# A first FFN product in 26 block products with streamed weight sums

## The chip, the cores and the metric

The kernel runs on one core of a Trainium2 chip. The core has five queues that matter here: TensorE (PE, matmuls into PSUM), VectorE (DVE), ScalarE (ACT), GpSimd (POOL), and SyncE (SP), which issues nearly all of the DMAs. Each works through its own instructions in the order of the program, and semaphores tie them together. The metric is the device time of one execution in microseconds (us). Everything is computed in float32.

## The reference, cut to what matters

The block normalises x and adds an attention branch and a feed-forward branch to it:

```python
xn = _layernorm(x, axis=-1)                                  # x: 8 x 1024 x 256
qkv = (xn @ qkv_w + qkv_b).reshape(b, n, 3, 16, 16)
q, k = _l2norm(q), _l2norm(k)
kv = jnp.einsum('bhnd,bhne->bhde', k, v)
out = jnp.einsum('bhnd,bhde->bhne', q, kv)                   # no softmax
attn = out @ proj_w + proj_b
h = jax.nn.relu(jnp.einsum('bsh,hi->bsi', xn, W1) + b1)      # W1: 256 x 1024
ffn = jnp.einsum('bsi,ih->bsh', h, W2) + b2                  # W2: 1024 x 256
return x + attn + ffn
```

The change is about h = relu(xn @ W1 + b1), which has 1024 tokens, 256 inputs and 1024 outputs in each of eight batches.

## The kernel before, in words

The eight batches go through a pipeline. For batch b the program does four things on TensorE, one after the other:

- `hidden(b)` (L646) forms h. This product and most of the others are done by a scheme of the Strassen and Winograd kind: a product of 2 x 2 blocks is formed from seven block products in place of eight. The blocks of x are two halves of the inputs by two halves of the tokens, `xnT`, plus the sums s1, s2 and s4 in `xS` and s3, which is formed in place (L221). The weights are `w1_sb` and their sums `w1t`. Four groups of 128 + 128 outputs, seven products each, make 28 block products of 512 columns a batch (L658). VectorE adds partial products from PSUM (L670), ScalarE applies relu with the bias (L665), GpSimd then forms the sums of h that the next product needs (`sums_of_a`, L190).
- `project_by_sums(b + 1)` (L399) forms q and k of the next batch in 14 block products of two 256-column matmuls each (`pqa`, `pqc`, `pqd`, `pqe`, L415).
- `second(b)` (L789) forms the output: seven products of five matmuls each, over the four groups of h and, as a fifth, the attention branch folded to a 256 x 256 matrix M times q. Results go through VectorE (`join`, `turn_back`) and are added to the rows of x in `xq` by GpSimd (L821), which SyncE then stores.
- Between the first four and the last three products of `second(b)` stands `mix_g_by_sums(b + 1)` (L577; `gpa`, `gpc`, `gpd`, `gpe`), the product of x and k of the next batch. Its sums are formed by GpSimd in `g_sums` (L545), in three parts.

Two small products, `mix_kv` (L613, `kvp`) and `mix_m` (L632, `mp`), stand inside `hidden`.

While that goes on, batch b + 2 is prepared: `norm_stats`, `norm_scale`, `norm_apply` (L274, eight instructions on ScalarE) and `turn_x` (L302), which transposes x with four 32 x 32 block transposes on VectorE and 16 DMAs on SyncE. `turn_q` (L494) does the same for q. Both use one buffer named turn. `norms_of_q` (L473) forms the norms of q and `scale` (L486) applies them.

The order is written by hand: `tc.manual_schedule()` keeps every engine's instructions in the order in which the Python code emits them, and a small table (`later_steps`, L760) says behind which step of `hidden` other work is emitted. The framework adds the waits. SyncE's queue follows that order too. Before, it ran in each batch: 16 DMAs of `turn_x`, eight stores, eight loads of `xq`, two loads of x, 16 DMAs of `turn_q`.

Seven PSUM banks are shared by all products (`bank`, L90), an eighth serves the small products.

## Time and profile before

| | |
|---|---|
| runs shown | 611.4, 611.2 and 610.72 us, median 611.2 |
| span of the profiled execution | 608.3 us |
| what lies around the span | 2.4 to 3.1 us, taken from the runs (the profiled execution's own time is not listed apart from its span) |
| TensorE busy | 604.2 us, 99% of the span |
| VectorE, ScalarE, GpSimd busy | 419.8, 208.0, 422.1 us |
| DMA | 45.42 MB, 75 GB/s on average |
| granted TensorE clock | 1.000 |
| one batch in the middle | 74.2 us (from 251.91 to 326.08), of which `hidden` 25.8 |

The stages of batch 3 on TensorE, read from the chain of work in order of time: `hidden` from 251.91 to 277.70, `project_by_sums(4)` to 289.79, the first four products of `second(3)` to 306.96, the mix of batch 4 to 313.21, the last three products to 326.08. In a line of the profile, `x10` counts instructions, two for each float32 matmul; "SPq" marks DMA issues on SyncE's queue; a time in square brackets is what the engine waited before and for whom.

### The profile page before, as it was taken

Reading aid. Unit: us, or ns where it says so; the run is one execution under the profiler, and the core shown is the slowest. Engines: PE = TensorE matmul, PEld = TensorE weight load, DVE = VectorE, ACT = ScalarE, POOL = GpSimd, SP = SyncE. Lnnn points to the kernel's source line nnn. Section 1 sums busy time; section 2 is a strip of 40 time slices with the busy share of each in tenths; the row PEclk is TensorE's granted clock in tenths of the full one; section 3 lists DMA queues with packets and bytes.
Section 4 is the critical chain, followed back from the end, with each engine's and each line's share of the span. In section 5 each row is a group of like instructions: output and inputs, shape, how many; then the busy total and the mean of one; then the engine's idle time right before and its main releaser. Section 6 shows DMA issues by size and latency. Waiting matters only on the chain.

```text
span 608.3 us, 6773 instructions
## 1 busy us (share of the span) xinstructions
PE 604.2 (99%) x2049; PEld 349.1 (57%) x2049; DVE 419.8 (69%) x754; ACT 208.0 (34%) x362; POOL 422.1 (69%) x346
## 2 busy tenths in 40 slices
PE   9999999999999999999999999999999999999998
PEld 5466664565644756447464484644846447554446
DVE  6987667877487774787647875577846878257854
ACT  4644214441334413343133531435205262023500
POOL 2899992699636995479944899249991599923900
PEclk9999999999999999999999999999999999999999
DMA  8543403840048300581005810159001550005313
GB/s 287 88 101 75 99 1 71 167 108 0 1 98 190 59 1 2 120 185 41 0 13 127 178 31 0 24 118 193 13 0 36 128 114 1 1 1 123 84 21 84
DMA packets 150068, 45.42 MB, mean 75 GB/s; under 512 B 145936, under 2 KB 147088, under 8 KB 150032
## 3 DMA queue, kind: packets, MB, share of 16 engines
q1 hardware_dynamic: 146528, 43.84, 32.4%
q10 hardware_dynamic: 3504, 1.15, 0.8%
q8 instruction: 16, 0.26, 0.2%
q14 instruction: 20, 0.16, 0.1%
HBM read 20.32 MB, written 8.39 MB: 47 GB/s over the span
## 4 chain that ended last, share of the span: by engine, by line
PE 99%; DVE 0%; issue 0%
PE poa L784 11%; PE poe L784 11%; PE pod L784 10%; PE pha L658 9%; PE phe L658 9%; PE phd L658 9%; PE poc L784 6%; PE phc L658 5%; PE pqd L415 4%; PE pqe L415 4%; PE pqa L415 4%; PE pq L326 2%; PE gpd L588 2%; PE gpe L588 2%; PE gpa L588 2%; PE pqc L415 2%
## 5 line engine op out<-in xcount | busy, mean ns | idle before, releaser
L821 POOL TENSOR_TENSOR xq<-xq,yt_o 128x512 f32<-128x512 f32 x29 | 36.8, 1269 | 119.5 <-DVE yt_o L816 119.5
L665 ACT ACTIVATE hT<-hT,b_sb 128x512 f32<-128x512 f32 x96 | 69.0, 722 | 61.3 <-DVE hT L670 56.2
L192 POOL TENSOR_TENSOR hS<-hT 128x512 f32<-128x512 f32 x31 | 46.5, 1500 | 32.5 <-ACT hT L665 32.5
L658 PE MATMUL pha<-xnT,w_sb 128*128 128x512 f32 x128 | 65.4, 592 | 0.0
L393 ACT ACTIVATE sq<-qk 128x512 f32<-128x512 f32 x56 | 34.2, 627 | 83.8 <-DVE qk L421 69.2
L784 PE MATMUL poa<-hT,w_sb 128*128 128x512 f32 x128 | 57.6, 592 | 0.0
L670 DVE TENSOR_TENSOR hT<-phe,u 128x512 f32<-128x512 f32 x64 | 43.7, 685 | 7.0 <-PE phe L658 5.2
L194 POOL TENSOR_TENSOR hS<-hT,hS 128x512 f32<-128x512 f32 x31 | 39.6, 1276 | 2.4
L193 POOL TENSOR_TENSOR hS<-hS,hT 128x512 f32<-128x512 f32 x31 | 39.5, 1274 | 2.4
L196 POOL TENSOR_TENSOR hT<-hT 128x512 f32<-128x512 f32 x31 | 39.9, 1289 | 0.0
L784 PEld LDWEIGHTS poa<-hT,w_sb 128*128 128x128 f32 x128 | 23.8, 190 | 24.2 <-issue 23.9
L658 PEld LDWEIGHTS pha<-xnT,w_sb 128*128 128x128 f32 x128 | 23.7, 190 | 22.9 <-issue 22.2
L670 DVE TENSOR_TENSOR u<-phc,u 128x512 f32<-128x512 f32 x32 | 21.7, 679 | 20.2 <-ACT u L684 11.0
L665 ACT ACTIVATE hT<-pha,b_sb 128x512 f32<-128x512 f32 x32 | 21.8, 683 | 35.5 <-PE pha L658 35.5
L816 DVE STREAM_TRANSPOSE yt_o<-y_o 128x512 f32<-128x512 f32 x29 | 31.7, 1093 | 2.9 <-ACT y_o L953 0.6
L658 PE MATMUL phc<-xS,w1t 128*128 128x512 f32 x64 | 32.7, 592 | 0.0
L658 PE MATMUL phd<-xnT,w_sb 128*128 128x512 f32 x64 | 32.7, 592 | 0.0
L658 PE MATMUL phd<-xnT,w1t 128*128 128x512 f32 x64 | 32.7, 592 | 0.0
L658 PE MATMUL phe<-xS,w_sb 128*128 128x512 f32 x64 | 32.7, 592 | 0.0
L658 PE MATMUL phe<-xS,w1t 128*128 128x512 f32 x64 | 32.7, 592 | 0.0
L684 ACT COPY u<-pha 128x512 f32<-128x512 f32 x32 | 18.4, 575 | 35.5 <-PE pha L658 35.5
L784 PE MATMUL poe<-hS,w2t 128*128 128x512 f32 x64 | 28.8, 592 | 0.0
(192 smaller groups left out, 1323.3 us busy)
## 6 DMA issues: line engine op xcount, KB each, us to landing
qT<-turn_q SPq DMA_DIRECT2D x128, 64.0 KB, 2.1
x<-in_L_attn_x_dram SPq DMA_DIRECT2D x15, 512.0 KB, 5.6
xq<-in_L_attn_x_dram SPq DMA_DIRECT2D x60, 128.0 KB, 3.7
out_dram<-xq SPq DMA_DIRECT2D x58, 128.0 KB, 2.7
xnT<-turn_x SPq DMA_DIRECT2D x112, 64.0 KB, 2.1
w_sb<-in_L_ffn_W_dram SPq DMA_DIRECT2D x2, 512.0 KB, 7.1
w_sb<-in_L_ffn_W_dram SPq DMA_DIRECT2D x8, 128.0 KB, 3.5
x<-in_L_attn_x_dram SPq DMA_DIRECT2D x3, 256.0 KB, 6.0
```

Source lines behind the costliest of these rows:

```text
L192: eng.tensor_tensor(s1, a21, a22, ALU.add)
L193: eng.tensor_tensor(s2, s1, a11, ALU.subtract)
L194: eng.tensor_tensor(s4, a12, s2, ALU.subtract)
L196: eng.tensor_tensor(a21, a11, a21, ALU.subtract)
L393: nc.scalar.activation(sq, part_of_qk(b, n, g, m), AF.Square)
L415: nc.tensor.matmul(dst[:, w, :], a[:, g, :, w], rhs, start=start and w == 0, stop=stop, skip_group_check=True,)
L588: nc.tensor.matmul(dst, l[:, t, :], r[:, t, :], start=start and t == 0, stop=stop and t == HT - 1, skip_group_check=True,)
L658: nc.tensor.matmul(dst, lhsT, rhs, start=start, stop=stop, skip_group_check=True)
L665: nc.scalar.activation(block(i, n, m), src, AF.Relu, bias=b1_sb[:, fc : fc + 1])
L670: nc.vector.tensor_tensor(dst, p, q, ALU.add)
L784: nc.tensor.matmul(dst, l, r, start=start and n == 0, stop=stop and n == len(lhs) - 1, skip_group_check=True,)
L821: nc.gpsimd.tensor_tensor(xh, xh, yt.rearrange("p u w r c -> p (u w) r c"), ALU.add)
```

## The change

For batches 1 to 7 the first FFN product is computed by another scheme. W1 is cut into four blocks of 256 outputs by two of 128 inputs, x into two blocks of 128 inputs by four of 256 tokens; the 4 x 2 x 4 block product takes 26 block products, where 28 were used. A block product is now two matmuls of 256 columns, one for each 128 outputs. The table `PRODUCTS` lists, for each, the PSUM chain into which it is added, the sum of W1 blocks, and the sum of x blocks; `STEPS` lists in which order products, copies out of PSUM (ScalarE), additions (VectorE) and relus (`"R"`, ScalarE, two instructions each) are emitted. A chain's bank is read between its products, with the partial sum in it, and later products are added on top.

The 26 sums of W1 are formed once, during `second(0)`, on VectorE (19) and ScalarE (2), and stored in DRAM by 26 DMAs. From then on they are streamed: 13 pairs of 256 KB a batch, through five places in SBUF, ten products ahead at the start of `hidden` and the rest within it. The sums of x are formed by GpSimd: ten while `hidden` of the batch before runs, eight more (X3 to X10, kept in the place of k) after the mix. q and k are projected from seven of the same sums and the blocks of x, which needs three more sums of their weights. Batch 0 keeps its old scheme under the name `first_hidden`.

What else moves: in `second`, the products come in the order a, a, f, c, d, then the mix, then e, e, so that two products stand behind the mix where there were three; `join(1, 1)` stands behind the turn of x; `join(1, 0)` is emitted ahead of the last part of `g_sums`; the sums of h and q are formed after the whole of `hidden`; the loads of `xq` and x stand behind `hidden`; half of the stores move into the next batch's `hidden`. The bias of q and its scaling go from GpSimd and `hidden` into `norms_of_q` on VectorE, which moves ahead of the c product (for batch 1 it stays behind the turn of x).

The core of the diff:

```diff
+PRODUCTS = (
+    (23, "+21-22-31+32", "s3B"), (20, "+21", "b12"), (24, "+12", "b22"), (8, "+11", "b12"),
+    (1, "+22", "b22"), (24, "-12-21+41-42", "X3"), (4, "+21-22-41+42", "X1"),
+    (10, "+12+42", "s1A"), (11, "+41-42", "X2"), (7, "+12+32+42", "b23"),
+    (10, "-12-31-42", "s2A"), (11, "+21-41+42", "X4"), (12, "+31-32", "dA"),
...
+    (3, "-42", "X9"), (2, "+21-41", "X10"),
+)
+STEPS = (
+    0, 1, ("copy", 42, 20, 1), 2, ("add", 24, 42, "-", "B23"), ("copy", 12, 24, 1), 3, 4,
...
+    ("add", 41, "B11", "+", 41), ("R", 41), 16, ("add", 23, 23, "+", "B12"), ("copy", 14, 8, 1),
+    ("R", 23), 17, ("add", 34, "B3", "-", 14), 18, ("add", 32, "B1", "+", 34), ("R", 32), 19,
+    ("add", 24, "B12", "+", 24), ("R", 24), 20, ("add", 34, "B12", "+", 34), ("R", 34), 21,
...
+)
     def sums_of_wqk():
...
+        for dst, p, q in (
+            (wt[:, 0, :], b12, b11), (wt[:, 1, :], b22, wt[:, 0, :]), (t3, b22, b12),
+            (wt[:, 2, :], b21, wt[:, 1, :]), (wts["t1"], b22, b21), (wts["t2"], b12, wts["t1"]),
+        ):
+            nc.gpsimd.tensor_tensor(dst, p, q, ALU.subtract)
...
     def norms_of_q(b):
...
+        for u in (3, 0):
+            q1 = part_of_qk(b, u, 0)
+            nc.vector.tensor_tensor(
+                q1, q1, dbias.unsqueeze(1).to_broadcast([P, 2, C]), ALU.add
+            )
...
+            scale(nc.vector, b, h, 0)
...
+    def make_forms(f, names):
+        for v in names:
+            p, op, q = FORMS[v]
+            nc.gpsimd.tensor_tensor(f[v], f[p], f[q], ALU.add if op == "+" else ALU.subtract)
+
+    def sums_of_x(b):
+        make_forms(
+            forms_of(b), ("s3B", "s1A", "s2A", "dA", "s4A", "s1B", "s2B", "s4B", "X1", "X2")
+        )
...
+    def load_w1(n, m):
+        if n % 5 == 4:
+            dst = w1_pair(n)
+        else:
+            flat = w1_sb.rearrange("p k (n s t c) -> p (k n s) t c", s=2, t=2, c=P)
+            dst = flat[:, 2 * (n % 5) : 2 * (n % 5) + 2 * m]
+        nc.sync.dma_start(out=dst, in_=w1f[:, 2 * n : 2 * (n + m)])
...
+    def hidden(b):
...
+            w = w1_pair(n // 2)[:, n % 2]
+            for t in range(2):
+                nc.tensor.matmul(
+                    banks[chain][:, t], w[:, t, :], f[v], start=start and t == 0,
+                    stop=n == last[chain], skip_group_check=True,
+                )
...
     def later_steps(b):
...
+        steps[2] += [lambda: store(b - 1, 0)]
+        steps[3] += [lambda: load_w1(5, 2), lambda: mix_kv(b)]
+        steps[7] += forms("s1A") + [lambda: load_w1(7, 2), lambda: turn_q(b)]
+        steps[9] += [lambda: mix_m(b), lambda: load_w1(9, 1), lambda: turn_q(b)]
...
+        steps[13] += forms("s4A", "X1") + [lambda: load_w1(10, 2), lambda: turn_q(b)]
+        steps[15] += [lambda: load_w1(12, 1), lambda: turn_q(b)]
...
     def second(...):
...
+        a = po("a")
         product(a, b11, a11, True, False)
         u1 = tmp("u1")
         nc.scalar.copy(u1, a)
         early()
+        product(a, b21, a12, False, True)
+        y = tmp("y")
+        nc.scalar.activation(y, a, AF.Identity, bias=ob[:, 2, 0:1])
+        mid()
         turn_back(0, 0, y)
+        f = po("f")
+        product(f, t4, a22, True, True)
+        c_ = po("c")
+        product(c_, t2, s2, True, True)
+        u2 = add(tmp("u2"), c_, u1)
+        d = po("d")
+        product(d, t3, s3, True, True)
+        u3 = add(tmp("u3"), d, u2)
+        join(1, 0, f, u3)
+        between()
+        yield
+        e = po("e")
+        product(e, t1, s1, True, False)
+        join(1, 1, e, u3)
+        store(b, 1)
         product(e, b22, s4, False, True)
         join(0, 1, e, u2)
         yield
...
         next(out_parts)
         if b + 1 < B:
             mix_g_by_sums(b + 1)
+            more_sums_of_x(b + 1)
         if b + 2 < B:
             norm_apply(b + 2, range(NT))
             for _ in range(R):
                 turn_x(b + 2)
-        if b + 1 < B:
-            norms_of_q(b + 1)
+        if b == 0:
+            norms_of_q(1)
         next(out_parts)
```

`between` is the last part of `g_sums`, `early` the statistics of batch b + 2, and `mid` is `norms_of_q(b + 1)` (for batch 0 the second half of the sums of W1 and the first load of weights).

## The prediction

> **What bounds the kernel now.** I read the page first (busy shares and the chain), then the chain in order of time for one batch, then the queues around the places that the change touches.

> ```profile
> PE 604.2 (99%) x2049; PEld 349.1 (57%) x2049; DVE 419.8 (69%) x754; ACT 208.0 (34%) x362; POOL 422.1 (69%) x346
> PE 99%; DVE 0%; issue 0%
> ```

> TensorE (PE) is busy from end to end and the chain is PE alone: no other queue holds it up. Time comes off only where PE has less to do, and goes on wherever PE has to wait. The chain for batch 3, in order of time (start, length, what):

> ```profile
> 236.36 0.89 PE gpa L588 x8
> ...
> 239.04 4.29 PE poa L784 x10
> ...
> 251.91 0.86 PE pha L658 x2
> ...
> 277.70 0.86 PE pqa L415 x4
> 278.57 0.86 PE pqe L415 x4
> ```

> A matmul leaves two records. Ten at 512 columns take 4.29, so a block product of `hidden` (two) takes 0.858; four at 256 columns take 0.8635 (the distance from pqa to pqe is 0.87, 14 of them take 12.09). `hidden` lasts 25.8, from 251.91 to 277.70: 28 x 0.858 + 0.89 (kvp) + 0.86 (mp).

> Two more stretches matter. SyncE's queue (SP), whose order is fixed, and ScalarE (ACT) and VectorE (DVE) at the end of batch 2:

> ```profile
> 242.35 10.47 SPq L295 DMA_DIRECT2D xnT<-turn_x  x16
> 252.92 5.38 SPq L830 DMA_DIRECT2D out_dram<-xq  x8
> 260.54 5.29 SPq L112 DMA_DIRECT2D xq<-in_L_attn_x_dram  x8
> 265.95 1.02 SPq L103 DMA_DIRECT2D x<-in_L_attn_x_dram  x2
> ```

> ```profile
> 237.45 4.04 ACT L279 ACTIVATE x<-x,nmr,rstd 128x256 f32<-128x256 f32 x8
> ...
> 241.58 2.49 DVE L293 STREAM_TRANSPOSE turn_x<-x 128x512 f32<-128x512 f32 x4 [2.21 <-ACT x L279]
> 243.99 2.62 DVE L394 TENSOR_REDUCE ssq<-sq 128x32 f32<-128x512 f32 x4
> ```

> An issue on SP takes 0.65 whether it carries 64 or 128 KB. 5.1 pass from the end of the second gpa product (237.25) to the first DMA of the turn of x (a copy, eight normalisations, one transpose). The two loads of 512 KB in that stretch landed late:

> ```profile
> DMA to landing us min/median/max: 5.0/5.8/6.6
> ```

> **The change, part by part.** I call the start of `hidden` T0 and its products 0 to 25.

> *PE work.* 26 x 4 records of 256 columns are 26 x 0.8635 = 22.45, against 24.03: 1.58 less in each of seven batches, **-11.05**. All other PE work keeps its records.

> *Weights through SP.* The first ten products find theirs loaded. Products 10 to 13 wait for load_w1(5, 2), which in SP's order stands behind 16 DMAs of the turn of x, four of store(b-1, 1), four of store(b-1, 0). From the end of the second gpa product: 5.1 to the first turn DMA, 10.47 + 0.10 for sixteen, 5.38 for the stores, so issue at 21.05. Its landing time L is unknown. Bounds: 3.6 (2.1 for a 64 KB turn, plus 512 KB at the 300 GB/s that the trace reaches at 270 us, 1.75) and 6.6 (the second of the pair above); I take 4.5, near the 5.0 of the first, because eight slower reads stood in front of that one. PE needs the weights after 2 x 0.89 (rest of the kv mix) + 8.58 (e, now the only output product behind the mix) + 10 x 0.8635 + 0.89 + 0.86 = 20.75. Before, 12.87 stood where 8.58 stands, and nothing urgent stood behind the stores. So PE waits 21.05 + 4.5 - 20.75 = 4.8, in batches 2 to 6: **+24.0** (3.9 to 6.9 each). Behind this wait on SP stand load_w1(7, 2), four turns of q and so on; product 14 comes 3.45 later, the second load lands about 2 later: covered. load_w1(10, 2) waits for product 13 and has products 14 to 19, 5.2, for a landing of about 4.5: covered, by 0.7 only. Batch 7 has no turn of x in front: the load is issued 5.9 after T0 (the store waits until 3.2 for join(0, 1): 0.75 + 1.10 + 1.27), lands at 10.4 and is needed at 10.4: 0.

> Inside the same stretch are two waits that this chain swallows: join(1, 1) now follows the transposes of x on VectorE, so e's second half starts 1.5 late (transposes end 6.82 after the gpa product, 0.75 for the join, against 6.07); and the last kv products wait for t4, which GpSimd (POOL) now forms behind join(1, 0): 0.69 + 0.75 + 1.10 + 1.27 + 1.28 + 0.3 of handovers = 5.4 after the d product, needed at 4.46, and s4 1.27 later. That is 0.95 + 0.4; only in batch 7 does it count by itself: **+1.3** (0 to 2.5).

> *Norms of q, batch 1.* In second(0), norms_of_q(1) still stands on VectorE between the transposes and join(1, 1), and now carries the bias (2 x 0.69) and the scaling (2 x 1.215). The first half of e ends at 6.07, the join at 6.82 + 1.4 + 0.6 (squares wait for the bias) + 4.1 (243.99 to 248.2, reduces to reciprocal) + 2.4 + 0.75 = 16.1. PE waits **10.0** (7 if the squares overlap, 12 if not at all); behind it stand the rest of e and `hidden`, and it delays T0 so far that the weights of batch 1 land in time.

> *Sums for q and k of batch 1.* GpSimd ran without a gap here:

> ```profile
> 40.59 0.74 POOL L188 TENSOR_TENSOR wt<-wqkv_sb,wt 128x256 f32<-128x256 f32 x1
> ...
> 53.43 1.28 POOL L229 TENSOR_TENSOR xS<-xnT 128x512 f32<-128x512 f32 x1
> ```

> Two more sums of weights (0.69 each) move the start from 53.4 to 54.8; s1B is the sixth form, 6 x 0.69 later, 58.9. PE asks for it at 55.7, with the whole projection behind it: **+3.2** (0 to 5).

> *Inside hidden.* Relu, once 0.72 for 512 columns, becomes two instructions of 256; eight 128x256 activations took 4.04, 0.505 each, so I take 0.47 (bounds 0.36 and 0.59), 15 us of ScalarE for 16 blocks. The copy of block 14 stands behind the relu of 41. With product 10 starting at 0: add 41 ends at 6.9, relu 7.9, copy 8.5, add 34 on VectorE 9.2, and product 20, which adds to the bank that add 34 reads, was due at 8.64: 0.65 in batches 2 to 6. Where no load wait lets VectorE catch up (it reaches product 10 some 1.3 late: 25 adds of 0.69, four transposes, two joins, M and kvm in 24.2 us) 1.2, batches 1 and 7: **+5.7** (0 to 12).

> *At nothing:* the loads of xq and x, moved behind `hidden` (5.3 + 1.0 of SP), have 12.1 of projection and 8.6 of output products before the first join reads them, and the ten first weights behind them have some 45; the 18 forms (0.69 each) fit between the mix and the sums of h; the sums, scaling and k sums (26.4 + 3.8 + 5.0) end 32 after `hidden`, the mix starts at 33.5 (uncovered, each us late is one lost); the weight forms of batch 0 (19 VectorE instructions of about 0.41, 26 stores of some 0.6 on SP) end before the c product and the turn of x. q and k keep 28 x 2 products, the output 35.

> Sum: -11.05 + 24.0 + 10.0 + 3.2 + 1.3 + 5.7 = +33.2. The profiled execution has a span of 608.3, and the median of the runs, 611.2, lies 2.9 above it; I keep that difference: 608.3 + 33.2 + 2.9 = **644.4, say 644**.

> [...] Here sixteen starts took 10.47 against 2.1 for one landing; with starts at nothing the load would be early, the sum 24 lower and the time about 620. [...]

> **Rivals.**
> *Slower PE after each gap.* For it: the first fifteen matmuls of 128 columns took 3.41, 0.227 each, against 0.11 for kvp later. Against: the granted clock is shown as 1.00 there too. If PE ran at that half rate for as long as those fifteen, a gap costs half of 3.4: six times 1.7, 654.6.

> *The loads are early enough.* This needs the 24 starts in front to take 0.465 each or less ((20.75 - 5.1 - 4.5) / 24); the two x loads took 0.43 to 0.54, the turns and stores 0.61 to 0.66. Then join(1, 1) still costs 1.5: 644.4 - 24.0 + 5 x 1.5 = 627.9.

> *Not slower.* Both large waits come from the turn of x and what follows it standing ahead of join(1, 1) and the stores. If that block began 10 us earlier, both would be gone: 611.2 - 11.05 + 3.2 + 1.3 + 5.7 = 610.4, and under 611 if relu is at its low end. Place: ScalarE's eight normalisations. Point: from 10 us of lead on. Against: in the trace they begin 0.16 after the gpa copy begins, and they still follow that copy.

> **How the numbers follow.** As forecast 0.59, slower PE 0.16, loads early 0.15, not slower 0.10 (0.07 faster, 0.03 the same; 0.2% is about what runs of this kernel can tell from no change). Slower 0.90. The forecast's own range is 633 to 660: the load 3.9 to 6.9 gives -4.5 and +10.5, the waits inside `hidden` about 6 either way, the rest 3 to 5. The range reaches down past the early loads (628 less 6) and up past the slower PE (655 and 13): 622 to 668.

> **What would show it.** PE's share falls to about 93%; product 10 (the first behind mp) waits for the weights' DMA about 4.8 in batches 2 to 6 and not in 1 and 7; e's second half in batch 0 waits about 10 for VectorE; the first pqe waits about 3 for GpSimd; product 20 waits under 1 for VectorE; `hidden` without its waits lasts 24.2. I am wrong if SP reaches the load before T0 + 6, if GpSimd's sums run past the mix, or if VectorE paces all of `hidden`.

## The result, and the profile after

The changed kernel takes 689.2 us (median of four runs, 687.1 to 690.1) against 611.0 us before (610.2 to 611.4): 1.128 times as long, 95% interval 1.126 to 1.130. The prediction was 644 us, with a range of 622 to 668. The direction was right; of 78 us I had seen 33. The span of the profiled execution is 687.7 us, 79.4 more than the 608.3 of before.

The page of the changed kernel, TensorE's busy time and the chain that ended last:

```profile
PE 622.3 (90%) x2385; PEld 423.1 (62%) x2385; DVE 487.5 (71%) x826; ACT 241.0 (35%) x504; POOL 469.8 (68%) x435
...
PEclk9998997799999999999999999998999999999999
...
DVE 25%; PE 23%; POOL 22%; DMA 8%; issue 7%; SPq 6%; ACT 5%; ACTq 1%; DVEq 0%; POOLq 0%
```

A chain that was PE alone is now spread over every queue. Busy time says less than it seems: TensorE has 11 us less to do and is "busy" 18 us longer, above all because some of its matmuls run at half speed (the 7s and 8s in the row of the clock; a short slow stretch in a slice of 17 us still shows as 9). Whom TensorE waits for (total us, times, longest):

```profile
PE ph L934 <- DMA w_sb<-w1f: 19.5, 9, 4.5
PE poe L1026 <- DVE y_o L1072: 13.1, 7, 8.1
PE pqe L513 <- POOL xS L317: 6.4, 1, 6.4
PE gpd L697 <- POOL gt L664: 6.3, 6, 1.1
PE gpa L697 <- ACT u_g L706: 6.1, 6, 3.6
PE poa L1026 <- ACT u_o L1186: 5.0, 7, 0.9
```

Those for `ph`, `poe` of batch 0 and `pqe` are in the prediction's sum, that for `gpd` is in its text as swallowed; `gpa` and `poa` are not in it. One batch shows where each stands. TensorE from the output of batch 2 into `hidden(3)` (start, length, what; in brackets the wait before it and for whom):

```profile
257.00 1.12 PE L1026 MATMUL poa<-qT,M 128*128 128x512 f32 x2 [0.68 <-ACT u_o L1186]
...
280.40 1.16 PE L697 MATMUL gpd<-gt,x 128*128 128x128 f32 x8 [1.05 <-POOL gt L664]
...
287.93 1.12 PE L1026 MATMUL poe<-hS,M 128*128 128x512 f32 x2 [0.84 <-DVE y_o L1072]
...
306.28 2.05 PE L934 MATMUL ph<-xS,w_sb 128*128 128x256 f32 x4 [3.40 <-DMA w_sb<-w1f]
308.12 1.79 PE L934 MATMUL ph<-qk,w_sb 128*128 128x256 f32 x4
309.74 1.03 PE L934 MATMUL ph<-w1t,w_sb 128*128 128x256 f32 x4
```

Product 10 (306.28) waits for the weights, as predicted. Then look at the distances: products 10 and 11 start 1.84 and 1.62 before the next one, all others 0.86. The granted clock and the busy times in three stretches of 3.41 us, the first in the wait and two behind it (columns: stretch, length, PE, PEld, DVE, ACT, POOL, each with its number of instructions, then clock, DMA share, GB/s):

```profile
302.82:306.23 3.41, 0.06 (x1) 0.00 (x0) 1.90 (x4) 0.00 (x0) 2.17 (x4) 1.00 0.96 280
306.24:309.65 3.41, 3.37 (x8) 2.78 (x9) 0.69 (x1) 0.00 (x0) 0.73 (x1) 0.50 1.16 220
309.65:313.06 3.41, 3.41 (x17) 3.00 (x17) 2.94 (x5) 1.24 (x3) 2.01 (x3) 1.00 0.43 66
```

The clock is 0.50 in exactly the second of them.

The load itself, on SyncE, is where the prediction's chain put it, behind sixteen starts of the turn of x and eight stores:

```profile
284.41 11.60 SPq L381 DMA_DIRECT2D xnT<-turn_x  x16
296.11 5.38 SPq L1033 DMA_DIRECT2D out_dram<-xq  x8
301.59 1.14 SPq L858 DMA_DIRECT2D w_sb<-w1f  x2
```

To add up the 79.4 I counted, for every pair of neighbouring TensorE records, how much later the second starts than at the usual distance (0.216 for 256 columns, 0.429 for 512, 0.112 for 128). That puts the half speed and the restart after a wait (0.24 to 0.27 where no half speed follows) beside the wait that caused them:

| place | predicted | measured, of it idle |
|---|---|---|
| less work on PE | -11.05 | -11.0 |
| batch 0: second block of the projection | 3.2 | 8.9, 6.4 |
| batch 0: mix of batch 1 | 0 | 6.8, 3.6 |
| batch 0: second half of e | 10.0 | 10.6, 8.1 |
| product 10 in batches 2 to 6 | 24.0 | 28.3, 18.1 |
| mix of batches 2 to 7 | 1.3 (the rest swallowed) | 14.0 |
| second half of e, batches 1 to 6 | swallowed | 6.7 |
| second half of a, all batches | 0 | 7.5 |
| inside `hidden`, batches 1 and 7 (2 to 6) | 2.4 (3.3) | 2.4 (0) |
| end: e and the last tokens | 0 | 4.0 |
| sum | +33.2 | +78.2; the other 1.2 lie in the start and in small waits |

### The profile page after: what moved, and what is told of

The parts are those of the page before. It is cut to its first block, busy times and chain, and to the rows that moved or that the text cites. A ratio compares the mean times of both kernels' runs of the same rounds, so it can differ in the third digit from the quotient of the medians.

```text
span 687.7 us, 7927 instructions
## 1 busy us (share of the span) xinstructions
PE 622.3 (90%) x2385; PEld 423.1 (62%) x2385; DVE 487.5 (71%) x826; ACT 241.0 (35%) x504; POOL 469.8 (68%) x435
## 4 chain that ended last, share of the span: by engine, by line
DVE 25%; PE 23%; POOL 22%; DMA 8%; issue 7%; SPq 6%; ACT 5%; ACTq 1%; DVEq 0%; POOLq 0%
PE ph L934 14%; PE poe L1026 6%; DMA w_sb<-w1f 6%; POOL qk L598 4%; POOL gs L664 4%; DVE qk L519 4%; SPq L381 3%; DVE hT L953 3%; DVE u_q L519 3%; POOL hT L242 2%; DVE st L341 2%; POOL hS L240 2%; ACT hT L961 2%; POOL qk L664 2%; SPq L1033 2%
## 5 line engine op out<-in xcount | busy, mean ns | idle before, releaser
L961 ACT ACTIVATE hT<-hT,b_sb 128x256 f32<-128x256 f32 x224 | 96.3, 498 | 92.4 <-DVE hT L953 91.8
L953 DVE TENSOR_TENSOR hT<-ph,hT 128x512 f32<-128x512 f32 x84 | 56.3, 684 | 30.7 <-ACT hT L948 29.0
L953 DVE TENSOR_TENSOR hT<-hT,ph 128x512 f32<-128x512 f32 x77 | 52.1, 679 | 32.1 <-PE ph L934 28.6
L934 PE MATMUL ph<-xS,w_sb 128*128 128x256 f32 x140 | 39.4, 416 | 18.8 <-DMA w_sb<-w1f 18.8
L934 PE MATMUL ph<-qk,w_sb 128*128 128x256 f32 x196 | 52.6, 406 | 0.6 <-DMA w_sb<-w1f 0.6
L934 PE MATMUL ph<-xnT,w_sb 128*128 128x256 f32 x224 | 52.9, 379 | 0.0
L934 PEld LDWEIGHTS ph<-xnT,w_sb 128*128 128x128 f32 x224 | 42.0, 190 | 5.4
L934 PEld LDWEIGHTS ph<-qk,w_sb 128*128 128x128 f32 x196 | 39.6, 205 | 8.8 <-issue 1.9
L934 PEld LDWEIGHTS ph<-xS,w_sb 128*128 128x128 f32 x140 | 28.1, 205 | 25.3 <-issue 19.9
L1026 PEld LDWEIGHTS poa<-hT,w_sb 128*128 128x128 f32 x128 | 24.2, 190 | 30.8 <-issue 30.1
L242 POOL TENSOR_TENSOR hT<-hT 128x512 f32<-128x512 f32 x29 | 39.0, 1345 | 0.0
L1072 DVE SCALAR_TENSOR_TENSOR y_o<-poe,ob,u_o 128x512 f32<-128x512 f32 x14 | 10.5, 750 | 35.5 <-PE poe L1026 35.5
L1026 PE MATMUL poe<-hS,w_sb 128*128 128x512 f32 x64 | 30.1, 614 | 0.0
L598 POOL TENSOR_TENSOR qk<-qk,ssk 128x1024 f32<-128x1024 f32 x14 | 29.9, 2155 | 0.0
```

The costliest lines, as they stand in the source:

```text
L242: eng.tensor_tensor(a21, a11, a21, ALU.subtract)
L598: eng.tensor_tensor(part, part, norms_of[b, h, s].unsqueeze(3).to_broadcast([P, HT, H, D]), ALU.mult,)
L934: nc.tensor.matmul(banks[chain][:, t], w[:, t, :], f[v], start=start and t == 0, stop=n == last[chain], skip_group_check=True,)
L953: nc.vector.tensor_tensor(block(v), operand(p), operand(q), ALU.add if op == "+" else ALU.subtract)
L961: nc.scalar.activation(part, part, AF.Relu, bias=b1_sb[:, fc : fc + 1])
L1026: nc.tensor.matmul(dst, l, r, start=start and n == 0, stop=stop and n == len(lhs) - 1, skip_group_check=True,)
```

## The experiments

Each is an edit of the changed kernel. Ratios are against the kernel before, whose median was 610.3 to 610.9 beside them; the changed kernel stands at 1.128.

### Is the half speed caused by the wait?

```diff
                     small()
+                if step == 9 and 1 < b < B - 1:
+                    spare = ps_mix.tile([P, C], F32, tag="mix", name=f"spare_{b}")
+                    for n in range(12):          # 6 in the second run
+                        nc.tensor.matmul(
+                            spare, ident, projw_sb[:, n % 2, :], start=True, stop=True,
+                            skip_group_check=True,
+                        )
```

> In batches 2 to 6, twelve matmuls of 256 columns into a spare bank stand ahead of product 10, 2.6 us of work in the 3.4 to 4.5 us in which PE waits for the weights; the weights arrive as late as before. Theory (a wait of 3.4 us or more makes PE run at half rate afterwards): products 10 and 11 take 1.73 and not 3.46, hidden in these batches lasts 27.8 and not 29.5, 5 x 1.7 = 8.5 less, about 680 to 681. Rival (the first products after the load are slow for another reason, the load's own traffic for one): 689, and products 10 and 11 still take about 3.46.

692.9 us, 1.134 (1.132 to 1.137), neither account. Products 10 and 11 took 0.87 each, but I had forgotten that a float32 matmul leaves two records: twelve of them are 5.2 us of work, not 2.6, and outlasted the wait. Half as many:

> Six matmuls of 256 columns (twelve records, 2.6 us) ahead of product 10 in batches 2 to 6, where twelve took 5.2 and outlasted the wait. Theory (products 10 and 11 run at half rate because PE stood still for 3.4 us or more): no still time over 1.2 us, products 10 and 11 take 0.87 each, hidden lasts 27.8 and not 29.5, 5 x 1.7 = 8.7 less than the changed kernel, 680 to 681. Rival (another cause): 689.

680.8 us, 1.115 (1.112 to 1.118): where the theory put it. The same place in batch 3:

```profile
301.90 2.86 PE L948 MATMUL spare<-projw_sb,ident 128*128 128x256 f32 x12 [0.78 <-DVE M L749]
304.59 1.03 PE L934 MATMUL ph<-xS,w_sb 128*128 128x256 f32 x4
305.46 1.03 PE L934 MATMUL ph<-qk,w_sb 128*128 128x256 f32 x4
```

The weights arrive as late as before, TensorE does useless work meanwhile, and the kernel is 8.4 us faster. The half speed follows from standing still; in the changed kernel it costs 9.4 in `hidden` and 7.7 in batch 0 (2.4 behind the projection's wait, 3.0 in the mix, 2.3 in e). Both theories gave 3.4 us as the least wait that does it, and that was not shown: at product 10 of batch 6 of the changed kernel a wait of 3.16 was enough. The last section shows shorter ones, and what the half speed went with in these traces.

### Is the load late through SyncE's order?

First the two loads were started by ScalarE (`nc.scalar.dma_start` in `load_w1(5, 2)` and `load_w1(7, 2)`).

> The loads of weight pairs 5 and 6, and 7 and 8, are started by ScalarE's queue and not by SyncE's. Theory (the load is late only because SyncE reaches it late, and PE then runs its first two products at half rate): the 5.1 to 7.2 us that product 10 loses in each of batches 2 to 6 go, hidden there lasts 25.4 as in batch 1 and not 29.5 to 31.5, the time falls by about 23 to 666. Rival one (the half rate does not come from the wait): only the waits of 3.4 to 4.5 go, hidden lasts 27.1, 674 to 675. Rival two (the transfer itself is slow beside the turn of x, wherever it is started): 687 to 690.

707.4 us, 1.159 (1.157 to 1.161), outside all three. TensorE still waits at product 10, now for VectorE, and SyncE waits for the loads that it no longer starts. Waits of the TensorE queue and of SyncE's:

```profile
PE ph L934 <- DVE hT L953: 21.5, 6, 4.7
```

```profile
SPq L381 <- DMA w_sb<-w1f: 34.3, 7, 6.8
...
SPq L1033 <- DMA w_sb<-w1f: 17.3, 6, 8.5
```

The trace shows why: its records give, for every DMA that SyncE or ScalarE starts, the semaphore on which the landing is counted, and both queues use the same eight (numbers 101 and 104 to 110; in the trace of the changed kernel they take all 506 starts of SyncE and all 19 of ScalarE). In this stretch a start waits for the semaphore on which it will itself be counted; in the changed kernel 490 of SyncE's 506 do. The fourteenth start of the turn of x in batch 3 had semaphore 101, as had ScalarE's load; it stood from 300.2 to 305.8, until that load had landed. The turn of x then left the buffer named turn late, VectorE's transpose of q waited 4.4 for it, and the additions behind it kept product 10 waiting. The run says nothing on the order on SyncE; that took another edit, which only moves the stores on that queue:

```diff
-        steps[2] += [lambda: store(b - 1, 0)]
-        steps[3] += [lambda: load_w1(5, 2), lambda: mix_kv(b)]
-        steps[7] += forms("s1A") + [lambda: load_w1(7, 2), lambda: turn_q(b)]
+        steps[3] += [lambda: load_w1(5, 2), lambda: mix_kv(b), lambda: store(b - 1, 1)]
+        steps[7] += forms("s1A") + [
+            lambda: load_w1(7, 2), lambda: store(b - 1, 0), lambda: turn_q(b)
+        ]
...
         join(1, 1, e, u3)
-        store(b, 1)
```

> On SyncE the four stores of each half of the output stand behind a load of weights (the loads of pairs 5 and 6, four stores, the load of pairs 7 and 8, four stores), nothing else is moved. Theory (the load is late because SyncE reaches it 5.4 us of stores too late): SyncE starts the load about 3.8 after hidden begins and not 9.3, it lands at 8.5 to 9, product 10 is due at 10.4 and does not wait, hidden in batches 2 to 6 lasts 25.4 as in batch 1, 5 x 4.6 = 23 less, 666. Rival (SyncE's next transfers then wait for the loads, VectorE's turn of q waits for those, and PE for VectorE): hidden 27 or more, 674 to 700.

689.8 us, 1.127 (1.121 to 1.134): no change at all. The time lies in the rival's range, but neither account was right: TensorE doesn't wait for VectorE. In batch 3 product 10 no longer waits (306.00), and ten products later stands a wait of the same size:

```profile
306.00 1.03 PE L934 MATMUL ph<-xS,w_sb 128*128 128x256 f32 x4
...
318.75 1.62 PE L934 MATMUL ph<-qk,w_sb 128*128 128x256 f32 x3 [3.70 <-DMA w_sb<-w1f]
```

That is product 20, whose load (pairs 10 and 11) SyncE started at 313.70, behind two sets of q's transfers that the stores had pushed back. The prediction had called this load "covered, by 0.7 only". So the loads of pairs 9 to 12 were put ahead of the last three quarters of q's transfers as well, with VectorE's transposes left in place:

```diff
-        steps[15] += [lambda: load_w1(12, 1), lambda: turn_q(b)]
+        steps[15] += [lambda: load_w1(12, 1), lambda: turn_q(b), move_q]   # starts the 12 transfers of q kept back
```

> The edit of the stores (behind the loads of pairs 5 to 8), and in addition the loads of pairs 9 to 12 ahead of the transfers of the last three quarters of q on SyncE; VectorE's transposes of q stay where they are. Theory (every one of the five late loads of a batch was late in SyncE's order, first the load for product 10, and with that mended the load for product 20): no wait for weights over 0.5 us in batches 1 to 7, hidden 25.3 to 25.6 there, 7 batches at 29.1 to 30.4 become 25.4, 31 less than the stores alone, 659; against the changed kernel 5 x 4.4 = 22 less, 667. Between these, 658 to 668. Rival (512 KB need longer than a ring of five slots leaves them, whatever the order): hidden 27 to 30, 675 to 690.

666.8 us, 1.092 (1.090 to 1.094), as the theory had it (658 to 668), though one wait of 1.0 was left where it had none over 0.5. `hidden` lasts 24.7 to 26.0 in batches 1 to 7; of the waits for weights, 2.2 us are left in the whole execution. SyncE in batch 3, whose turn of x ends at 290.2 and whose `hidden` begins at 287.5:

```profile
291.11 0.33 SPq L865 DMA_DIRECT2D w_sb<-w1f  x1
291.53 2.93 SPq L1041 DMA_DIRECT2D out_dram<-xq  x4
295.45 0.33 SPq L865 DMA_DIRECT2D w_sb<-w1f  x1
```

Moving the stores behind two loads, and twelve transfers of q behind the rest, is worth 22 us. Streaming the weights through five places is possible almost without a wait, if no store and no transfer of q that can come later stands in front of a load on SyncE.

### The order of the output products, and what VectorE does ahead of the mix

The order of before (a, c, d, e, then the mix, then a, e and d again, which takes the place of f) in the changed kernel, with a store behind the load:

```diff
+        product(c_, t2, s2, True, True)        # from a, a, f, c, d | mix | e, e
+        u2 = add(tmp("u2"), c_, u1)            # to a, c, d, e | mix | a, e, d (second half for f)
         early()
+        product(d, t3, s3, True, False)
+        u3 = add(tmp("u3"), d, u2)
+        mid()
+        between()
+        product(e, t1, s1, True, False)
+        join(1, 1, e, u3)
+        yield
         product(a, b21, a12, False, True)
...
+        product(d, t4, a22, False, True)
+        join(1, 0, d, u2)
```

> The output products stand in the order of the kernel before: a, c, d and the first half of e ahead of the mix; the second half of a, the second half of e and f behind it. The store that follows the last join stands behind the load of pairs 5 and 6. Theory (the new order costs twice: each second half follows its first at once and waits for the reader of the bank, and 4.3 us less work covers SyncE's queue): no wait for the copy of a (0.84 a batch) nor for the join of e (1.11), product 10 waits 0 to 1 us, batch 0 loses its 10.5 at e: 28 + 6.7 + 5.9 + 10.4 = 51 less, 638; up to 7 more where VectorE, which has the norms of q ahead of the mix and three joins behind it, is late (638 to 645). Rival (VectorE is the bound and takes it back in the mix or in hidden): 655 or more, with waits for VectorE of 2 us or more in each batch in their place.

683.9 us, 1.121 (1.116 to 1.127): the rival. The waits at a and e are gone but for batch 7, of those for the loads 4.4 are left, `hidden` lasts 25.1 to 27.0, but the mix lasts 13.8 to 18.2 where it lasted 8.2 to 13.1:

```profile
PE gpa L697 <- ACT u_g L706: 44.7, 7, 9.2
```

The copy `u_g` needs the buffer of `join(1, 1)`, and that join now stands on VectorE behind the norms of q. The same norms were tried with their scaling of q behind the last join ahead of the mix (`scale` moved from `norms_of_q` to `between`):

> VectorE's scaling of q (two instructions, 4.3 us beside GpSimd's sums) stands behind the last join ahead of the mix and not in front of it, from batch 2 on. Theory (the mix waits because VectorE reaches that join late): the waits in the mix of batches 2 to 7, 1.9 to 3.0 each, fall to 0.3 to 0.6, about 10 less, 679. Rival (the join is bound by PE's last product ahead of it, whatever VectorE did before): 688 to 690, the mix still takes 8.2 to 9.2.

687.2 us, 1.126 (1.120 to 1.131), not to be told from the changed kernel. The join came only 0.5 us earlier, since d had just ended (the rival's point), the waits for `u_g` in batches 2 to 7 did go, and a longer one took their place, because VectorE now scaled q while GpSimd formed t4. In batch 4 (VectorE and GpSimd):

```profile
359.41 3.40 DVE L603 TENSOR_TENSOR qk<-qk,ssq 128x1024 f32<-128x1024 f32 x2
...
361.70 2.25 POOL L669 TENSOR_TENSOR gt<-qk,gs 128x512 f32<-128x512 f32 x1
...
363.91 1.27 POOL L669 TENSOR_TENSOR gs<-x,gs 128x512 f32<-128x512 f32 x1
```

An addition of GpSimd takes 1.27 alone and 2.25 beside these. In batches 2 to 7 the mix now waits 16.5 for `gt` (t4), where the changed kernel waited 6.3. What in the two instructions makes them slow each other no run shows; the rows show that moving work between or along these two queues is no free move.

### Batch 0

The reload of half of W1 was started inside `hidden`, the first eight weight forms were put ahead of the projection's additions on VectorE, `sums_of_x(1)` ahead of `g_sums(1, 0)` and `sums_of_h` on GpSimd, and `norms_of_q(1)` into `mid`, ahead of the mix:

```diff
-        of_h = {3: (0,), 6: (1,), 11: (2, 3)}
+        of_h = {3: (0,), 11: (1, 2, 3)}
...
+            next(of_w1)
             project_by_sums(1, [lambda: turn_q(0), last_turn])
...
-        if b == 0:
-            norms_of_q(1)
```

> Batch 0 alone is rearranged: the reload of half of W1 is started inside hidden, the first eight weight forms stand on VectorE ahead of the projection's adds, GpSimd's sums of x stand ahead of its sums for g and of its sums of h, and the norms of q of batch 1 stand ahead of the mix as in the other batches. Theory (batch 0 loses 8.9 at the sums, 6.8 in the mix and 10.5 at e only through that order): the second block of the projection waits 0 to 2 us, e waits 1.1, the mix loses 2 to 4 because VectorE still reaches the last join late: 20 less, 669. Rival (VectorE and GpSimd slow each other where both have much to do, so that the forms make GpSimd's sums late and the waits only change place): 675 to 690, with instructions of VectorE at 1 us and more for 256 elements there.

680.6 us, 1.114 (1.110 to 1.119), in the rival's range: of 20 us, 8.6 came. The second block of the projection no longer waits and e loses 1.1, but the fourth block waits 4.0 for VectorE, the output 2.5 for q's transfers (now behind the stores of the forms), and the mix loses 7.9. The weight forms have changed their victim. What one costs is seen in the changed kernel itself, in batch 0 (busy time and count of each engine in two stretches; order of columns as above):

```profile
76.30:94.00 17.70, 17.02 (x41) 7.35 (x40) 16.96 (x18) 1.53 (x3) 16.79 (x12) 1.00 0.22 73
94.00:101.30 7.30, 7.30 (x36) 4.67 (x35) 6.79 (x28) 1.60 (x4) 0.00 (x0) 1.00 0.28 94
```

In the first stretch GpSimd is busy for 16.79 of the 17.70 us and VectorE ends 18 instructions in 16.96 us of work; in the second GpSimd is idle and VectorE ends 28 in 6.79. Ten of the 19 weight forms ran while GpSimd was idle, and each took 0.42; eight of the nine beside GpSimd took 1.37 to 2.15. One group of them (least, median and most, in ns):

```profile
L881 DVE TENSOR_TENSOR xnT<-xnT,w_sb x7: 420/426/2151, 85.8 to 100.6; 128x256 f32<-128x256 f32 x7
```

### All orders together

The edits to batch 0 and to the stores, the output as a, c, a, d, the mix, then e, f, e, GpSimd's last sums for g ahead of all joins, and the scaling of q between the first two joins behind the mix:

> The edits to batch 0, the stores behind the loads, and a new order of the output products: a, c, the second half of a, d ahead of the mix; e, f, the second half of e behind it; the scaling of q stands on VectorE between the first two joins behind the mix, GpSimd's last sums for g ahead of all joins. Theory (the time was lost to orders and not to work): hidden 25.4, mix 6.3 to 7, no wait inside the output, batch 0 loses 2 at the sums of x and 3 in its mix, the tail 4: 608.3 - 11.05 + 7 x 1.2 + 7 x 0.4 + 9 + 2.9 = 620 (612 to 630). Rival (VectorE and GpSimd together are the bound and give the waits back elsewhere): 640 or more.

657.0 us, 1.076 (1.074 to 1.078), in the rival's range, but not by the rival's cause. Everything named in the output went (mix 6.25 to 6.5 in batches 2 to 7, no wait at a or e before batch 7), batch 0 lost 20, and `hidden` still lasted 27.4 to 30.1, by the load for product 20. With the loads ahead of q's transfers, q of batch 0 turned ahead of the forms, six forms there and the first join ahead of the norms:

> All orders as in the run of that name, with the loads ahead of q's transfers, q of batch 0 turned ahead of the weight forms, six forms there for eight, and in batch 0 the first join ahead of the norms of q. Theory: hidden falls from 27.4 to 30.1 to 25.4 in seven batches, 25 less; batch 0 loses 2 to 4 at the projection's fourth block where it lost 5.9, nothing for q where it lost 6.7, 0 to 3 in its mix where it lost 7.5: 12 less; 657 - 37 = 620 (614 to 630). What then remains over 597 (608 less 11) would be VectorE's: 1.2 in each hidden, 6 to 10 in batch 0, 3 at the end. Rival (the waits come back behind VectorE): 635 or more.

642.4 us, 1.053 (1.050 to 1.057), the fastest with the 26 products, and still 32 us slower than before. That is the rival's range, though TensorE waits mainly for GpSimd and not for VectorE. `hidden` lasts 24.7 to 25.9, as expected. What TensorE waits for now:

```profile
PE poc L1035 <- POOL hS L239: 10.0, 6, 7.3
PE gpd L703 <- POOL gt L670: 3.8, 6, 1.1
```

Its span, 638.9, is 42 over the 597 that less work on TensorE alone would give: 18 of these lie between `hidden` of batch 0 and that of batch 1, 13 in the output and the mix of batches 1 to 6, 6 in `hidden`, 3 in the output of batch 7 and behind it. The first row is new: c reads GpSimd's sums of h, and with everything else earlier, GpSimd is late. Two more orders were tried against that, d ahead of c, and f ahead of c with all joins behind the mix:

> As the last of the combined orders, with d ahead of c, so that PE asks for GpSimd's sums of h one product (4.3 us) later; nothing else is moved. Theory (the combined order now waits for GpSimd, which has no gap from the end of hidden to the mix): c's waits of 0.4 to 0.9 in batches 1 to 6 go and 4.3 of the 9.7 in batch 0, 8 less, about 634, while the mix still waits about 1 for the last sums for g, since GpSimd ends them no earlier. Rival (the order of the products alone made the wait, GpSimd has room): the mix's waits for GpSimd go too, 6 more less, 628 or lower.

701.9 us, 1.149 (1.147 to 1.151). My premise was wrong: d reads `hT`, and its last piece is the one that GpSimd writes last (17.9 us in six waits, and in batch 0 9.9 for the last piece of `qT`), so that moving d forward made it worse, and the join behind the later a held up the mix (24.5).

> The edits to batch 0, to the stores, loads and transfers of q as in the second of the combined runs, and the output products in the order a, f, c, d ahead of the mix and e, the second half of a, the second half of e behind it, so that the two products that read GpSimd's sums of h (c, and d, whose operand GpSimd writes last) stand last ahead of the mix; all joins stand behind the mix, GpSimd's last sums for g right behind the others, the norms of q of batch 1 behind the joins. Theory (with the weights on time what is left is the order against GpSimd's sums, which last from the end of hidden to the mix): no wait at c or d in batches 1 to 6, the mix 6.3 to 6.8, 13 less than the second combined run there; batch 0 waits 3 at c for 9.7 and pays 3 to 5 in the next hidden for VectorE, 4 to 6 less: 642 - 18 = 624 (616 to 632), still slower than before. Rival (GpSimd's sums themselves are too long, in whatever order): the waits for GpSimd stay at 1 to 2 a batch, 635 or more.

663.6 us, 1.088 (1.084 to 1.092): the rival's range, but the waits are 2.3 to 3.2 a batch and stand at f, where neither account had one. In five of the six batches half speed follows:

```profile
PE pof L1035 <- POOL hT L242: 17.4, 6, 3.2
```

f is held until GpSimd's last write to `hT` (L242), though in the code that instruction writes the block a21 and f reads a22, which lies beside it in the same tile; whether this wait is needed no run shows. The changed kernel's own order of the output (a, a, f, c, d) gives GpSimd more time ahead of c and d, and is paid for with the waits at a and e. No order that was tried beats the kernel before.

## Why the prediction was right or wrong

The direction was right, and so was the largest single term's place. The steps that failed are *At nothing*, and leaving the half speed out of the sum, to a rival. Of the 45 us that the sum missed, 22 lie in waits that it had put at nothing, 14 in half speed behind the waits that it had, and 9 in a chain on SyncE that was longer than worked out; the other terms nearly cancel.

- *PE work*, -11.05: right. The products kept their distance of 0.86, and with the weights on time `hidden` lasts 24.7 at best against 24.2 worked out.
- *Weights through SP*, 4.8 in each of five batches: the mechanism, its place and its batches were right, and batch 1 and 7 were free of it; the term was too small. From the end of the second gpa product to product 10 it had 25.55; the five batches took 27.0 to 28.3, 27.4 on average. Of the 1.85, 0.95 is the queue (22.0 for 21.05; in two of five batches one start of the turn took 1.7 and 1.9 for 0.61) and 0.9 the landing (5.4, from the start of the load to product 10, for the 4.5 chosen between 3.6 and 6.6). The claim that this chain swallows the waits for t4 and at e held: product 10 came 3.8 late (3.6 idle and 0.2 of restart), not 6.65. Ahead of batch 7, where nothing swallows them, they cost 2.8, and 1.3 had been counted.
- *Slower PE after each gap*, the rival with a chance of 0.16: it came true together with the forecast. It was priced 10.2 for six gaps; eight gaps (five loads, three in batch 0) cost 17. I had let a clock of 1.00 at the first fifteen matmuls speak against it. But the trace of before has no record of the clock ahead of 5.13 us, behind those fifteen, and the view shows 1.00 where there is none; their own distance, 0.227 against 0.11, was the reading to go by.
- *Norms of q, batch 1*, 10.0: 10.6, of it 8.1 of waiting and 2.3 of half speed. The wait was where the prediction put it and 1.9 shorter; that the sum agrees is luck, since the half speed was not in it.
- *Sums for q and k of batch 1*, 3.2 between 0 and 5: 6.4 of waiting, and 2.4 of half speed behind it. The step counted two more sums of weights and missed a wait on GpSimd ahead of them. One of the new sums is kept in a buffer that VectorE still reads in the fold of the bias:

```profile
43.86 0.74 POOL L479 TENSOR_TENSOR t<-wqkv_sb 128x256 f32<-128x256 f32 x1 [3.37 <-DVE wqkv_sb L621]
```

- *Inside hidden*, 5.7: 1.1 and 1.2 in batches 1 and 7, where 1.2 was worked out; nothing in 2 to 6, where product 10's wait and half speed gave VectorE time.
- *At nothing* is the part that failed: 6.8 in the mix of batch 1, 7.5 at the second half of a, 4.1 at the second `gpa` of the later mixes, 4.0 at the end. The 19 forms on VectorE were counted at 0.41 and to end before c; beside GpSimd they took up to 2.15, the last ended at 101.3, within the mix, which lost 6.8. GpSimd's sums were to end 32 after `hidden`, 1.5 ahead of the mix; in batch 3 they ended at 356.7, 34.7 after it, largely because two of them took 2.25 beside VectorE. The `gpa` waits stand behind VectorE's joins and its scaling of q: with the scaling moved, those of batches 2 to 7 were gone. The order a, a was costed at nothing, and no step asked what stands between two products that share a bank: the second half now follows its first at once and waits for the copy, 0.68 to 0.90 idle and 0.26 of restart in every batch; with c between them (*All orders together*) that wait was gone. The order of the last output product was not looked at either (4.0).
- The rival *loads early enough* fell: 24 starts took 0.67 to 0.74 each, not 0.465. *Not slower* fell with it.

What the starts on SyncE cost decided the largest term: with the eight starts of the stores behind it (5.4 us), the load for product 10 was no longer late.

## What to carry to other kernels

When a kernel is bound by TensorE at 99%, every other queue has been fitted around it; an edit that takes 2% of the matmuls and adds 16% to VectorE and 11% to GpSimd is first of all a new schedule for those two, and the sum must price each of their instructions beside the other's, not alone (a weight form took 0.42 alone and up to 2.15 beside GpSimd). Give each queue its own list of what stands in front of the one urgent item, and after mending one item look at the next: here the same 5 us moved from product 10 to product 20. And add to a wait of some 3 us the half speed that can follow it, here 1.6 us and more, before believing that a wait is worth its own length.
